# Two-layer graph block on one core: a fused tail for one more batch, and reordered statistics in the last part

## The chip, the cores and the metric

The kernel runs on one core of one Trainium2 chip. The metric is the device time of one execution in microseconds (us). A core has five engines that work side by side, each through its own in-order list of instructions: TensorE (PE in the profile; its weight loads are listed as PEld), VectorE (DVE), ScalarE (ACT), GpSimd (POOL) and SyncE (SP), which here only issues DMAs. They meet through semaphores: an instruction waits until the data that it reads are written and the buffer that it writes has been read out, and everything behind it on the same engine waits with it.

## The reference, cut to what matters

The input x has 128 batches of 128 rows by 512 columns, all in float32. There are two layers, each followed by a residual sum and a normalization over the 512 columns.

```python
# layer 0
A = einsum('od,bdn->bon', adj, x);  C = A + b          # same matrix twice
x = layernorm(x + max_over_columns(relu(A[..., None, :] + (C - A)[..., :, None])))
# layer 1: attention with 8 heads of 64 over the 128 rows of a batch
q, k, v = split(x @ w_qkv)
p = softmax(where(adj == 0, -inf, q @ k.T / 8))
o = (p @ v) @ w_proj + b_proj
x = layernorm(x + o + layernorm(o) * ln_gamma + ln_beta)
```

`layernorm(y)` is `(y - mean) / sqrt(var + 1e-5)`. For one batch the end of layer 1, called the tail below, is therefore: statistics of o, the inner normalization times gamma, two sums (with o, and with the output of layer 0 to which beta has been added already), statistics of that sum z, the outer normalization, and the store.

## The kernel before

Batches are worked in pairs (p counts pairs) and groups of four (g). A loop runs over the first 60 pairs; the rest, from `first = qk_unit(NG - 1, 0)` at line 951 to line 1194, is written out by hand, batch by batch. In it L is 127, the last batch, and LQ is 63, the last pair. The change lies in this last part only. The order of the calls in the source is the order of the instructions on each engine (`pin` keeps it), so moving a call moves all its instructions, on every engine that it uses.

**Matrix products.** The products with w_qkv and w_proj are done as units of seven block products in place of eight (`Unit`), over four PSUM banks b1 to b4. `product(i)` is a run of 8 matmul records on TensorE into the bank of that product (1, 6 and 7 use bank 1; 2 bank 2; 3 and 5 bank 3; 4 bank 4). `snap(k)` copies bank 1 to SBUF on ScalarE (line 186), and `result(half, col)` adds a bank and a snapshot on VectorE (line 199). `result(0, 1)` and `result(1, 1)` read bank 3. The next unit's product 5 goes into bank 3 again, so it waits for `result(0, 1)` of the unit before, and `snap(2)` reuses a buffer that the same result reads. `relay` and `relayed` (lines 191, 194) are copies on ScalarE that stand for some of the results in the last units, and `seed` (line 526) puts a bias into a bank. For the last four batches, `last_project` multiplies by the plain w_proj into a PSUM tile `pp`, which is o of that batch.

**Attention.** `scores` (tile pss), `softmax_max` (lines 405 and 417 on VectorE), `softmax_exp` (line 424, ScalarE, eight heads), `prob_out` (line 435 reciprocal, a multiply recorded at line 77, the transpose at line 445, and a DMA to DRAM from SP), `prob_read` (the DMAs back, line 465), `attend` (tile po) and `attend_copy` (line 495, ScalarE).

**Four ways to do a tail.** `stats` makes mean and variance on VectorE (`bn_stats` line 255, `bn_aggr` line 256), a negated mean (line 267) for those items that are not `fused`, and on GpSimd the variance plus epsilon (line 269), its power of -1/2 and the shift (both line 77); `columns` is its VectorE half without line 267, `finish_stats` the rest. The plain tail of a batch is `tail_inner_one` (ScalarE, line 278), `tail_residual_one` (three GpSimd instructions on 128x512: times gamma, plus o, plus the rest), statistics of z, and `tail_outer_one` (ScalarE and the store from SP, line 637). `scalar_stats` does the statistics of z on ScalarE instead (lines 665, 666, 669: per batch a pass for the sum, one for the squares), with three small GpSimd instructions in `finish_scalar_stats`. The fused tail does the middle on VectorE:

```python
def fused_open(b, mean):
    z_tile(b)      # z = (o - mean) * gamma;  rest = o + rest
    scalar_tensor_tensor(zs[b], o_of(b), mean, ga_bc, subtract, mult)    # line 624
    tt(nc.vector, rs_[b], o_of(b), rs_[b], add)                         # line 77
def fused_close(b):   # z = z * rs + rest
    scalar_tensor_tensor(z, z, rs, rs_[b], mult, add)                    # line 632
```

Before the change, batches 120 (L-7), 124 (L-3), 125, 126 and 127 take the fused tail, 121 (L-6), 122 and 123 the plain one. The very last outer normalization runs on VectorE (`tail_outer_vector`, line 653). Line 77 is the helper `tt` and line 74 the helper for matmuls, so many operations share these lines and are told apart by their tiles: `zl` holds z of the late batches (`z` and `xr` for some), `early` and `wlast` hold the rest, `s_o` the block sums for the second unit of w_proj, `st_mv_last`, `mv_last`, `rs_mv_last` and `sh_mv_last` the statistics, and `su`, `me`, `de` those of `scalar_stats`.

Of the kernel before, what the change touches and what calls it, by code (L numbers as in the profile page):

```python
# [16 lines left out]
def kernel(  # L17
# [58 lines left out]
    def tt(eng, dst, a, b, op):  # L76
        pin(eng.tensor_tensor(dst, a, b, op))  # L77
# [180 lines left out]
    def finish_stats(mv, keys, fused=0):  # L258


        n = len(keys)
        if n == 0:
            return
        part = slice(fused, n)
        sh = small.tile([P, NC], F32, tag="sh", name=f"sh_{mv.name}")
        if n > fused:
            pin(nc.vector.tensor_scalar(sh[:, part], mv[:, part, 0], -1.0, None, ALU.mult))
        rs = small.tile([P, NC], F32, tag="rs", name=f"rs_{mv.name}")
        pin(nc.gpsimd.tensor_scalar(rs[:, :n], mv[:, :n, 1], EPS, None, ALU.add))  # L269
        tt(nc.gpsimd, rs[:, :n], rs[:, :n], mhalf.to_broadcast([P, n]), ALU.pow)  # L270
        if n > fused:
            tt(nc.gpsimd, sh[:, part], sh[:, part], rs[:, part], ALU.mult)
        for k, key in enumerate(keys):
            stat_of[key] = rs[:, k : k + 1], sh[:, k : k + 1]

    def normalize(dst, src, key):
        rs, sh = stat_of.pop(key)
        pin(nc.scalar.activation(dst, src, AF.Identity, bias=sh, scale=rs))  # L278
# [140 lines left out]
    def softmax_exp(b, heads=range(H)):  # L419
        if 0 in heads:  # L420
            psums[b] = small.tile([P, H], F32, tag="sums", name=f"sums_{b}")
        for i in heads:
            pin(
                nc.scalar.activation(  # L424
                    prob[b][:, i],
                    prob[b][:, i],
                    AF.Exp,
                    bias=nmax[b][:, i : i + 1],
                    accum_out=psums[b][:, i : i + 1],
                )  # L430
            )
# [92 lines left out]
    def seed(unit, bank):  # L524
        bias = {1: bp_bc[:, :HE], 3: bd}[bank].unsqueeze(1).to_broadcast([P, 2, HE])
        pin(nc.scalar.copy(unit.new_bank(bank), bias))
# [37 lines left out]
    def tail_reload_to(q, place):  # L564
        pin(nc.sync.dma_start(out=place, in_=spill.pop(q)))
        for j in range(2):
            rs_[2 * q + j] = place[:, j]
# [33 lines left out]
    def z_tile(b):  # L601
        q, j = divmod(b, 2)
        tag, bufs = {58: ("xt", 2), 59: ("xt", 2), 60: ("z", 1), 61: ("qk0", 2)}.get(q, ("xs", 1))
        if tag == "xs":
            zs[b] = sb.tile([P, D], F32, tag=f"xs{b - B + G + 1}", name=f"z_{b}")
            return
        if q not in ends:
            ends[q] = sb.tile([P, 2, D], F32, tag=tag, name=f"zl_{q}", bufs=bufs)
        zs[b] = ends[q][:, j]

    def tail_inner_one(b):
        z_tile(b)
        normalize(zs[b], o_of(b), ("o", b))

    def tail_residual_one(b, steps=range(3)):
        for k in steps:
            with_, op = ((ga_bc, ALU.mult), (o_of(b), ALU.add), (rs_[b], ALU.add))[k]
            tt(nc.gpsimd, zs[b], zs[b], with_, op)

    def fused_open(b, mean):  # L620

        z_tile(b)
        pin(
            nc.vector.scalar_tensor_tensor(
                zs[b], o_of(b), mean, ga_bc, ALU.subtract, ALU.mult
            )
        )
        tt(nc.vector, rs_[b], o_of(b), rs_[b], ALU.add)

    def fused_close(b):  # L630
        z, (rs, _) = zs[b], stat_of.pop(("o", b))
        pin(nc.vector.scalar_tensor_tensor(z, z, rs, rs_[b], ALU.mult, ALU.add))
# [6 lines left out]
    def columns(name, *items):  # L639

        mv = small.tile([P, NC, 2], F32, tag="mv", name=f"mv_{name}")
        for k, (kind, b) in reversed(list(enumerate(items))):
            bn({"o": o_of, "z": zs.get, "y": xs.get}[kind](b), mv, k)
        return mv, items

    def stats(name, *items, fused=0):
        stat = columns(name, *items)
        finish_stats(*stat, fused)
        return stat[0]
# [6 lines left out]
    def scalar_stats(*batches):  # L656

        n, name = len(batches), f"{batches[0]}"
        trash = psum.tile([P, D], F32, tag="pss0", name=f"trash_{name}")
        sums, mean, dev = (  # L660
            small.tile([P, NC], F32, tag=f"{t}1", name=f"{t}1_{name}") for t in ("su", "me", "de")
        )
        act = nc.scalar.activation
        for k, b in enumerate(batches):
            pin(act(trash, zs[b], AF.Identity, accum_out=sums[:, k : k + 1]))
        pin(act(mean[:, :n], sums[:, :n], AF.Identity, scale=-1.0 / D))
        for k, b in enumerate(batches):
            pin(
                act(
                    trash, zs[b], AF.Square, bias=mean[:, k : k + 1], accum_out=dev[:, k : k + 1]  # L670
                )
            )
        return batches, mean, dev

    def finish_scalar_stats(stat):
        batches, sh, rs = stat
        n = len(batches)
        pin(nc.gpsimd.tensor_scalar(rs[:, :n], rs[:, :n], 1.0 / D, EPS, ALU.mult, ALU.add))
        tt(nc.gpsimd, rs[:, :n], rs[:, :n], mhalf.to_broadcast([P, n]), ALU.pow)
        tt(nc.gpsimd, sh[:, :n], sh[:, :n], rs[:, :n], ALU.mult)  # L680
        for k, b in enumerate(batches):
            stat_of["z", b] = rs[:, k : k + 1], sh[:, k : k + 1]
# [98 lines left out]
    for p in range(LAST):  # L781
        g, ph = divmod(p, 2)
        a, b = 2 * p, 2 * p + 1
        first = v_unit(0) if p == 0 else qk_unit(g + 1, ph)
# [3 lines left out]
        mv = small.tile([P, NC, 2], F32, tag="mv", name=f"mv_{p}")  # L788
# [152 lines left out]
    L = B - 1  # L941
# [3 lines left out]
    def prob_out(b):  # L945
        softmax_div(b)
        prob_transpose(b)
        prob_write(b)


    first = qk_unit(NG - 1, 0)
    mv = small.tile([P, NC, 2], F32, tag="mv", name=f"mv_{LAST}")
# [53 lines left out]
    early = sb.tile([P, 4, D], F32, tag="x1T", name="early", bufs=2)  # L1006
    for q in range(2):
        tail_reload_to(LQ - 4 + q, early[:, ds(2 * q, 2)])
    for t in (L - 13, L - 12):
        bn(o_of(t), mv, len(keys))  # L1010
        keys.append(("o", t))
    first.product(3)
    first.result(0, 1)
    softmax_exp(L - 4)
    prob_out(L - 5)
    for t in (L - 15, L - 14):
# [12 lines left out]
    before, o_u, v_u = second, o_unit(NG - 3), v_unit(NG - 1)  # L1029
# [47 lines left out]
    softmax_exp(L - 1, range(4))  # L1077
    o_u.product(3)
    v_u.product(2)
    prob_out(L - 2)  # L1080
    o_u.result(0, 1)
    softmax_exp(L - 1, range(4, H))
    v_u.relayed()
    softmax_max(L)
    v_u.product(6)
    v_u.snap(2)
    for t in (L - 9, L - 8):
        tail_inner_one(t)
        tail_residual_one(t)
    softmax_exp(L)  # L1090
    v_u.product(5)
    v_u.product(7)
    v_u.snap(3)
    v_u.product(4)
    stats("last_2", ("o", L - 11), ("o", L - 10))
    prob_out(L - 1)


    o_u = o_unit(NG - 2)
# [11 lines left out]
    o_u.product(1)  # L1111
    o_u.relay()
    v_u.product(3)
    for t in (L - 11, L - 10):
        tail_inner_one(t)
    prob_out(L)
    v_u.result(0, 1)
    o_u.product(2)
    o_u.relayed()
    seed(o_u, 3)  # L1120
    o_u.product(4)
    o_u.product(6)
    o_u.snap(2)
# [28 lines left out]
    last_project(L - 2, wlast)  # L1152
    for t in (L - 5, L - 4):
        tail_inner_one(t)
    mv = stats("last_5", ("o", L - 7), ("o", L - 6), fused=1)
    attend_copy(L - 1)
    attend_copy(L)
    last_project(L - 1, wlast)
    last_project(L, wlast)
    tail_inner_one(L - 6)  # L1160
    stat = scalar_stats(L - 11, L - 10)
    tail_residual_one(L - 5, [0, 1])
    fused_open(L - 7, mv[:, 0, 0:1])
    mv = stats("last_6", ("o", L - 3), fused=1)
    fused_open(L - 3, mv[:, 0, 0:1])
    fused_close(L - 7)
    fused_close(L - 3)
    tail_residual_one(L - 5, [2])
    finish_scalar_stats(stat)
    for t in (L - 11, L - 10):  # L1170
        tail_outer_one(t)
    tail_residual_one(L - 4, [0, 1])
    mv = stats("last_7", ("o", L - 2), ("z", L - 3), ("z", L - 7), fused=1)
    fused_open(L - 2, mv[:, 0, 0:1])
    fused_close(L - 2)
    tail_residual_one(L - 4, [2])
    for t in (L - 7, L - 3):
        tail_outer_one(t)
    stat = scalar_stats(L - 5, L - 4)
    tail_residual_one(L - 6, [0])  # L1180
    mv = stats("last_8", ("o", L - 1), ("z", L - 2), fused=1)
    fused_open(L - 1, mv[:, 0, 0:1])
    fused_close(L - 1)
    tail_residual_one(L - 6, [1, 2])
    finish_scalar_stats(stat)
    for t in (L - 2, L - 5, L - 4):
        tail_outer_one(t)
    mv = stats("last_9", ("o", L), ("z", L - 1), ("z", L - 6), fused=1)
    fused_open(L, mv[:, 0, 0:1])
    for t in (L - 1, L - 6):  # L1190
        tail_outer_one(t)
    fused_close(L)
    mv = stats("last_10", ("z", L), fused=1)
# [42 lines left out]
```

## Time and profile before

| what | us |
| --- | --- |
| timed runs, median of 3 | 1959.66 |
| lowest and highest of them | 1959.43, 1960.28 |
| the profiled execution, device time | 1959.19 |
| its span, first to last instruction | 1957.4 |
| granted TensorE clock, mean over the span | 0.996 |

The profiled execution is 0.47 us below the median of the timed ones, and 1.8 us of its time lie outside the span. Times inside the trace count from the start of the span. A line of the timeline gives start, duration, engine, source line, operation, the tile written and those read with their shapes, and in brackets how long the engine had been idle and what released it. Durations of one execution repeat closely for the same shape, so a duration well above that of its siblings is itself a finding.

### The profile page before, as it was taken

To read this page: it belongs to the slowest core of one execution; us is meant where nothing else is said; L and a number is where in the kernel's file an instruction comes from. 1 tells how busy PE (TensorE), PEld (TensorE's weight loads), DVE (VectorE), ACT (ScalarE), POOL (GpSimd) and SP (SyncE) were. 2 spreads that over 40 slices of the span, in tenths; PEclk is the share of its full clock that TensorE was granted. 3 is DMA by queue.
4 is the path that set the end of the run, shared out by engine and by line. 5 is a ranking of instruction groups with operands and counts; after the bars stand their busy time and mean duration, and the time that the engine had idled before them with its cause. 6 is when DMAs were issued, how large, how long until landed. Compare 5 with 4: busy or idle time off the path is not lost.

```text
span 1957.4 us, 33035 instructions
## 1 busy us (share of the span) xinstructions
PE 1932.5 (99%) x11533; PEld 1635.9 (84%) x11533; DVE 1562.1 (80%) x2514; ACT 1065.3 (54%) x3094; POOL 1296.3 (66%) x821
## 2 busy tenths in 40 slices
PE   9999999999999999999999999999999999999996
PEld 6888888888888888888888888888888888888884
DVE  6767878778778788787787787887877878878786
ACT  3444655555545546555555465565554554655575
POOL 6336766767667676667676676766676766767748
PEclk9999999999999999999999999999999999999998
DMA  7747566576566665666765756757667657567464
GB/s 223 170 121 188 145 185 180 160 199 162 168 189 166 178 192 157 190 166 168 205 159 165 199 153 186 189 158 193 166 167 201 161 169 195 156 188 180 133 220 136
DMA packets 444934, 341.74 MB, mean 175 GB/s; under 512 B 276832, under 2 KB 378336, under 8 KB 444768
## 3 DMA queue, kind: packets, MB, share of 16 engines
q1 hardware_dynamic: 444336, 338.85, 64.0%
q8 instruction: 91, 1.49, 0.3%
q10 hardware_dynamic: 432, 0.79, 0.1%
q14 instruction: 75, 0.61, 0.1%
HBM read 172.82 MB, written 166.72 MB: 173 GB/s over the span
## 4 chain that ended last, share of the span: by engine, by line
PE 94%; DVE 3%; POOL 2%; ACT 1%; issue 0%; POOLq 0%; ACTq 0%; DVEq 0%
PE b_qk L74 39%; PE b_v L74 19%; PE b_o L74 18%; PE pss L74 6%; PE po L74 6%; PE pa L74 5%; POOL zl L77 1%; DVE s L77 0%; DVE pu L445 0%; ACT s L424 0%; DVE st_mv_last L255 0%; DVE amax L291 0%; POOL rs_mv_last L77 0%; POOL s_o L77 0%; DVE s L405 0%
## 5 line engine op out<-in xcount | busy, mean ns | idle before, releaser
L74 PE MATMUL b_qk<-s_x,wqk 128*128 128x256 f32 x2048 | 473.8, 379 | 1.6 <-DVE qk L199 1.4
L74 PEld LDWEIGHTS b_qk<-s_x,wqk 128*128 128x128 f32 x2048 | 388.8, 190 | 56.0 <-DVE qk L199 2.2
L424 ACT ACTIVATE s<-s,nmax 128x128 f32<-128x128 f32 x1024 | 396.1, 391 | 3.9 <-DVE nmax L417 3.9
L74 PE MATMUL b_qk<-x1T,wqk 128*128 128x256 f32 x1536 | 358.9, 383 | 0.1
L74 PEld LDWEIGHTS b_qk<-x1T,wqk 128*128 128x128 f32 x1536 | 286.6, 190 | 45.3 <-issue 1.0
L77 POOL TENSOR_TENSOR z<-z,ga_bc 128x1024 f32<-128x1024 f32 x58 | 164.6, 2838 | 167.9 <-ACT z L278 167.9
L269 POOL TENSOR_SCALAR rs_mv<-mv 128x6 f32<-128x6 f32 (+2 forms) x61 | 14.7, 241 | 386.7 <-DVE mv L256 386.7
L77 DVE TENSOR_TENSOR s<-s,rec 128x1024 f32<-128x1024 f32 x128 | 253.1, 1977 | 4.4
L186 ACT COPY u_qk<-b_qk 128x512 f32<-128x512 f32 x192 | 112.3, 585 | 242.7 <-PE b_qk L74 241.8
L74 PE MATMUL b_v<-wv,s_x 128*128 128x256 f32 x1024 | 237.0, 379 | 0.9 <-DVE o L199 0.9
L74 PE MATMUL b_o<-wp,s_o 128*128 128x256 f32 x992 | 229.4, 379 | 0.7 <-POOL s_o L77 0.7
L74 PEld LDWEIGHTS b_v<-wv,s_x 128*128 128x128 f32 x1024 | 194.4, 190 | 27.8 <-DVE o L199 1.3
L405 DVE SCALAR_TENSOR_TENSOR s<-pss,mask 128x512 f32<-128x512 f32 x256 | 164.3, 683 | 61.3 <-PE pss L74 61.2
L74 PEld LDWEIGHTS b_o<-wp,s_o 128*128 128x128 f32 x992 | 188.2, 190 | 26.9 <-POOL s_o L77 1.1
L199 DVE TENSOR_TENSOR qk<-b_qk,u_qk 128x512 f32<-128x512 f32 x256 | 168.0, 675 | 49.8 <-PE b_qk L74 45.8
L77 POOL TENSOR_TENSOR x<-x,be_bc 128x1024 f32<-128x1024 f32 x64 | 181.3, 2833 | 33.1 <-DVE rec L435 27.4
L424 ACT ACTIVATION_READ_ACCUMULATOR s<-s,nmax 128x1 f32 x1024 | 194.4, 190 | 0.0
L199 DVE TENSOR_TENSOR v<-b_v,u_v 128x512 f32<-128x512 f32 x127 | 86.2, 680 | 133.6 <-PE po L74 128.8
L186 ACT COPY u_o<-b_o 128x512 f32<-128x512 f32 x91 | 53.3, 585 | 241.8 <-PE b_o L74 241.8
L186 ACT COPY u_v<-b_v 128x512 f32<-128x512 f32 x95 | 55.6, 585 | 234.7 <-PE b_v L74 233.4
L74 PE MATMUL b_v<-wv,x1T 128*128 128x256 f32 x768 | 176.5, 379 | 0.0
L74 PEld LDWEIGHTS b_v<-wv,x1T 128*128 128x128 f32 x768 | 145.8, 190 | 32.3 <-issue 13.9
(128 smaller groups left out, 3399.2 us busy)
## 6 DMA issues: line engine op xcount, KB each, us to landing
hop<-pu SPq DMA_DIRECT2D x128, 512.0 KB, 3.7
pT<-hop SPq DMA_DIRECT2D x512, 128.0 KB, 3.7
spill<-x SPq DMA_DIRECT2D x64, 512.0 KB, 4.8
x<-in_x_dram SPq DMA_DIRECT2D x62, 512.0 KB, 4.5
xhop<-xt SPq DMA_DIRECT2D x248, 128.0 KB, 2.3
x1T<-xhop SPq DMA_DIRECT2D x248, 128.0 KB, 3.9
xr<-spill SPq DMA_DIRECT2D x59, 512.0 KB, 3.6
out_dram<-xr SPq DMA_DIRECT2D x58, 512.0 KB, 4.1
```

The source lines that it names most:

```text
L74: pin(nc.tensor.matmul(*args, **kwargs))
L77: pin(eng.tensor_tensor(dst, a, b, op))
L186: pin(nc.scalar.copy(t, self.banks[1]))
L199: nc.vector.tensor_tensor(self.out[half, col], self.banks[bank], self.snaps[k], ALU.add)
L269: pin(nc.gpsimd.tensor_scalar(rs[:, :n], mv[:, :n, 1], EPS, None, ALU.add))
L405: nc.vector.scalar_tensor_tensor(s[:, par], pss[b][par], SCALE, mask.unsqueeze(1).to_broadcast([P, NP, P]), ALU.mult, ALU.add,)
L424: nc.scalar.activation(prob[b][:, i], prob[b][:, i], AF.Exp, bias=nmax[b][:, i : i + 1], accum_out=psums[b][:, i : i + 1],)
```

## The change

The first edits are moves. In three places `result(0, 1)` or a statistic changes its place among the VectorE instructions; in one, two tail inners and residuals go ahead of `product(6)` and `snap(2)`; in one, `stats` is cut into `columns` and a later `finish_stats`. The second half rewrites the end: the batch with index L-6 = 121 (the 122nd) takes the fused tail, `scalar_stats` of batches 122 and 123 is done one batch at a time, the GpSimd steps of 122 and 123 are placed anew, and the statistics of z of 121 move from `last_9` to `last_8`. The statistics of the last two batches (o of 127, z of 126) thus stand alone in `last_9`. No function is new.

```diff
+    first.product(3)
+    first.result(0, 1)
     for t in (L - 13, L - 12):
         bn(o_of(t), mv, len(keys))
         keys.append(("o", t))
-    first.product(3)
-    first.result(0, 1)
     softmax_exp(L - 4)
...
     softmax_exp(L - 1, range(4))
     o_u.product(3)
     v_u.product(2)
+    o_u.result(0, 1)
     prob_out(L - 2)
-    o_u.result(0, 1)
     softmax_exp(L - 1, range(4, H))
     v_u.relayed()
     softmax_max(L)
-    v_u.product(6)
-    v_u.snap(2)
     for t in (L - 9, L - 8):
         tail_inner_one(t)
         tail_residual_one(t)
+    v_u.product(6)
+    v_u.snap(2)
     softmax_exp(L)
...
-    stats("last_2", ("o", L - 11), ("o", L - 10))
+    stat = columns("last_2", ("o", L - 11), ("o", L - 10))
     prob_out(L - 1)
...
     v_u.product(3)
-    for t in (L - 11, L - 10):
-        tail_inner_one(t)
+    finish_stats(*stat)
     prob_out(L)
     v_u.result(0, 1)
     o_u.product(2)
     o_u.relayed()
     seed(o_u, 3)
+    for t in (L - 11, L - 10):
+        tail_inner_one(t)
     o_u.product(4)
     o_u.product(6)
     o_u.snap(2)
...
-    mv = stats("last_5", ("o", L - 7), ("o", L - 6), fused=1)
+    mv = stats("last_5", ("o", L - 7), ("o", L - 6), fused=2)
     attend_copy(L - 1)
     attend_copy(L)
     last_project(L - 1, wlast)
     last_project(L, wlast)
-    tail_inner_one(L - 6)
     stat = scalar_stats(L - 11, L - 10)
-    tail_residual_one(L - 5, [0, 1])
+    tail_residual_one(L - 5, [0])
     fused_open(L - 7, mv[:, 0, 0:1])
-    mv = stats("last_6", ("o", L - 3), fused=1)
-    fused_open(L - 3, mv[:, 0, 0:1])
+    mv1 = stats("last_6", ("o", L - 3), fused=1)
+    tail_residual_one(L - 5, [1, 2])
+    fused_open(L - 3, mv1[:, 0, 0:1])
     fused_close(L - 7)
     fused_close(L - 3)
-    tail_residual_one(L - 5, [2])
     finish_scalar_stats(stat)
     for t in (L - 11, L - 10):
         tail_outer_one(t)
-    tail_residual_one(L - 4, [0, 1])
+    stat5 = scalar_stats(L - 5)
+    fused_open(L - 6, mv[:, 1, 0:1])
     mv = stats("last_7", ("o", L - 2), ("z", L - 3), ("z", L - 7), fused=1)
     fused_open(L - 2, mv[:, 0, 0:1])
+    fused_close(L - 6)
     fused_close(L - 2)
-    tail_residual_one(L - 4, [2])
+    tail_residual_one(L - 4)
     for t in (L - 7, L - 3):
         tail_outer_one(t)
-    stat = scalar_stats(L - 5, L - 4)
-    tail_residual_one(L - 6, [0])
-    mv = stats("last_8", ("o", L - 1), ("z", L - 2), fused=1)
+    mv = stats("last_8", ("o", L - 1), ("z", L - 2), ("z", L - 6), fused=1)
     fused_open(L - 1, mv[:, 0, 0:1])
     fused_close(L - 1)
-    tail_residual_one(L - 6, [1, 2])
-    finish_scalar_stats(stat)
-    for t in (L - 2, L - 5, L - 4):
+    finish_scalar_stats(stat5)
+    stat4 = scalar_stats(L - 4)
+    for t in (L - 6, L - 2, L - 5):
         tail_outer_one(t)
-    mv = stats("last_9", ("o", L), ("z", L - 1), ("z", L - 6), fused=1)
+    finish_scalar_stats(stat4)
+    mv = stats("last_9", ("o", L), ("z", L - 1), fused=1)
     fused_open(L, mv[:, 0, 0:1])
-    for t in (L - 1, L - 6):
+    for t in (L - 4, L - 1):
         tail_outer_one(t)
     fused_close(L)
```

## The prediction

> **What bounds the kernel now.** I read the page's shares and chain first, then the windows of the last 90 us, then the timeline around each edit, one engine at a time.
>
> ```profile
> PE 1932.5 (99%) x11533; PEld 1635.9 (84%) x11533; DVE 1562.1 (80%) x2514; ACT 1065.3 (54%) x3094; POOL 1296.3 (66%) x821
> PE 94%; DVE 3%; POOL 2%; ACT 1%; issue 0%; POOLq 0%; ACTq 0%; DVEq 0%
> ...
> 1900.00:1928.00 28.00, 27.27 (x175) 21.61 (x175) 23.63 (x41) 17.08 (x40) 26.05 (x26) 1.00 0.58 169
> 1928.00:1940.00 12.00, 11.62 (x46) 5.36 (x42) 8.53 (x16) 7.83 (x17) 10.85 (x17) 1.00 0.25 94
> 1940.00:1957.40 17.40, 0.00 (x0) 0.00 (x0) 10.26 (x22) 8.43 (x16) 10.08 (x15) 0.55 0.33 121
> ```
>
> TensorE carries 94% of the chain, so over most of the span only its waits can be gained. The end is another matter: GpSimd is busy 26.05 of 28 us from 1900 and 10.85 of 12 from 1928, and after 1940 TensorE has nothing left, while VectorE and GpSimd (10.26 and 10.08 of 17.40) hand statistics to each other. What the change can move is a few TensorE waits before 1915 and this exchange.
>
> ```profile
> 1866.81 0.66 DVE L199 TENSOR_TENSOR qk<-b_qk,u_qk 128x512 f32<-128x512 f32 x1
> 1867.52 1.99 PE L74 MATMUL b_qk<-s_x,wqk 128*128 128x256 f32 x8 [0.56 <-DVE qk L199]
> ...
> 1898.64 0.65 DVE L199 TENSOR_TENSOR o<-b_o,u_o 128x512 f32<-128x512 f32 x1
> 1899.35 0.92 PE L74 MATMUL b_v<-wv,s_x 128*128 128x256 f32 x3 [0.93 <-DVE o L199]
> 1899.38 0.58 ACT L186 COPY u_v<-b_v 128x512 f32<-128x512 f32 x1 [1.37 <-DVE o L199]
> 1899.87 0.82 ACT L278 ACTIVATE zl<-o,sh_mv_last,rs_mv_last 128x512 f32<-128x512 f32 x1
> ...
> 1900.76 1.27 POOL L77 TENSOR_TENSOR zl<-zl,ga_bc 128x512 f32<-128x512 f32 x1 [2.47 <-ACT zl L278]
> ...
> 1903.70 2.11 DVE L77 TENSOR_TENSOR s<-s,rec 128x1024 f32<-128x1024 f32 x1
> 1904.69 2.27 POOL L77 TENSOR_TENSOR zl<-zl,ga_bc 128x512 f32<-128x512 f32 x1
> ...
> 1914.53 0.70 PE L74 MATMUL b_o<-wp,s_o 128*128 128x256 f32 x2 [0.73 <-POOL s_o L77]
> ...
> 1932.97 1.75 DVE L632 SCALAR_TENSOR_TENSOR z<-z,rs_mv_last,wlast 128x512 f32<-128x512 f32 x1 [2.02 <-POOL rs_mv_last L77]
> ...
> 1947.15 0.69 DVE L255 BATCH_NORM_STATS2 st_mv_last<-zl 128x6 f32<-128x512 f32 x1 [2.50 <-POOL zl L77]
> ...
> 1953.85 0.55 DVE L653 TENSOR_SCALAR z<-z,mv_last,rs_mv_last 128x512 f32<-128x512 f32 x1 [1.01 <-POOL rs_mv_last L77]
> ```
>
> The reader should see three TensorE waits (0.56, 0.93, 0.73); a ScalarE copy that waits 1.37 for the same result and holds up the first tail inner, and so GpSimd; and two late VectorE waits for GpSimd, of which 2.50 is for z of batch 121. Durations also show a collision: the divide (`s<-s,rec`) takes 1.23 at 1896.21 but 2.11 beside GpSimd, and the GpSimd product behind it 2.27 in place of 1.27.
>
> **What the Trainium skill says.** "SBUF — State Buffer", section "SBUF: two separate sides", calls the port pair of VectorE and GpSimd "an exclusive lock, not a bandwidth split": a VectorE instruction with two SBUF inputs and a GpSimd instruction exclude each other for their whole length, whoever starts first. The trace agrees: 1903.70 plus 2.11 less 1.23 is 1904.58, where the GpSimd sum from 1903.46 ends (1904.73). Sums that read a PSUM tile (`pp`, 0.68) show no such delay. So closing a fused tail (`z,rs,rest`, all SBUF) excludes GpSimd, and for batch 121, whose o lies in SBUF, opening it should too.
>
> **The change part by part.** Each number is laid on the order of instructions per engine in the built program; all gains count from the trace of before.
>
> *First move: bank 3 result before two statistics (1865).* VectorE is free for it at 1865.28, and the product that it reads is the first half of the run of 16 matmuls at 1863.35 (3.62), so done at about 1865.2. TensorE's wait of 0.56 goes; the statistics come 0.6 later on VectorE but end at the same time. I see no later wait that takes it back: VectorE waits 2.12 for `pss` at 1881.37, ScalarE 2.91 before 1884.19, and both shift. Gain 0.56.
>
> *Second move: `o_u.result(0,1)` before the softmax output (1896), and tail inners before `snap(2)`.* The result starts at 1895.42 instead of 1898.64, so TensorE's 0.93 goes too. VectorE's sum of work is unchanged. ScalarE is free at 1898.01 less 0.56 = 1897.45; the shift of batches 118 and 119, its small power slowed to 1.73 by a divide before, still has to wait for one and comes at 1897.6. The first inner runs at 1897.63 instead of 1899.87, GpSimd's residuals start at 1898.52 instead of 1900.76: 2.24 earlier. The price: `snap(2)` is now behind two inners of 0.76, ends at 1899.73, and product 7 waits about 0.25.
>
> *Third: `finish_stats` of 116 and 117 behind the block sums, their inners behind `seed`.* GpSimd does six residuals from 1898.52 (about 1.35 each, one blocked by a divide for 1.1) until 1907.4, four `s_o` sums (the second blocked until 1909.65 by the last divide) until 1913.6, and three small steps (1.29) until 1914.9. The sum that product 6 awaits ends at 1910.9, before TensorE asks (1912.6), so the 0.73 goes. But the inners now start at 1914.96, not 1911.93, and ahead of the next `snap(2)`, which ends at 1917.08; product 7 of this unit needs it and starts at 1917.12 instead of 1917.99. Of the TensorE gain 0.87 is left, of GpSimd's 1.04 (residual of 116 at 1915.85 instead of 1916.89). Removing the shift multiply of `last_5` saves 0.2 more on GpSimd.
>
> *Fourth: the tail.* Removed: inner of 121 on ScalarE (0.82), three GpSimd residuals (1.27, 1.71, 1.27), VectorE's wait of 2.50. Added on VectorE: open 0.77, sum 0.68, close 0.77; on ScalarE one more mean (0.20); on GpSimd a second triple of small steps (about 1.1). My schedule: statistics of 120 and 121 ready at 1925.35, `last_6` at 1927.65; close 120 at 1929.1, close 124 blocked by a GpSimd sum until 1932.57 (before 1934.72); open 121 blocked again by the last residual of 122, ending 1934.27, its sum 1934.9; three statistics until 1937.2 (before 1937.05). So the 2 us won at close 124 pay for the new work, here. Then GpSimd, which before was busy with residuals of 123 and took this set only at 1938.50, is idle and starts it at 1937.3; close 121 follows at 1938.75 beside it, close 125 is blocked by the first residual of 123 until 1941.22 (before 1940.51); three statistics (now with 121) until 1943.55, close 126 ends 1945.77 (before 1944.65), two statistics until 1947.38. Here the 2.50 wait and one set of statistics are gone. GpSimd's two triples end at 1947.87, its step for 127 at 1948.95, close 127 1949.75, statistics 1950.68, last steps 1951.63, final instruction 1951.67 instead of 1953.85. Sum: 2.18 earlier. The stores on SP are six of the same size in nearly the old order; batch 121's leaves two places earlier, and the last one still follows VectorE, so they cost nothing.
>
> *Unknown: does opening 121 exclude GpSimd?* No row of before shows one squarely against a residual; at 1926.30 such an opening (0.77) overlaps a small GpSimd step that took its usual 0.22. Ends: 0 (it excludes, as in the sum) and 0.9 (no block at 1932.55). I take the middle, 0.45.
>
> Gain 2.18 + 0.45 = 2.6. Against the profiled execution that is 1959.19 - 2.6 = 1956.6; the median of the runs is 0.47 higher, so 1957.0.
>
> **The rivals.** *The whole lead survives.* If the last divide doesn't block the second `s_o`, the small steps end 1.2 earlier, `snap(2)` is in time, and TensorE and GpSimd keep about 2.1; with 0.9 for the opening, 2.2 + 1.2 + 0.9 = 4.3: 1955.4. For it: the blocks depend on tenths of a us. Against: the divide took 2.33 at 1908.41 before, so GpSimd is dense there. *The lead is eaten.* Later `snap(2)` and blocks on each divide leave 0.3 of 1.04, and the longer VectorE list in the tail is blocked once more (0.75): 2.2 - 0.75 - 0.75 = 0.7: 1959.0. For it: VectorE's statistics in the tail are no earlier in my schedule (1937.2 against 1937.05). *Slower: VectorE becomes the bound of the tail by port exclusion.* Place: from opening 121 to closing 125, five two-SBUF instructions against three residuals of 123. If the lead of 1.04 is lost and the sum and close of 121 each wait a full residual (1.1), 2.2 - 1.04 - 2.2 = -1.0: 1960.6. It decides once more than two further blocks of a residual's length fall on VectorE. Against: GpSimd's residuals of 123 stand behind the statistics that VectorE must finish first, so most of the time there is nothing to collide with.
>
> **How the numbers follow.** Forecast 0.45, own range 1955.9 to 1958.6; whole lead 0.28; eaten 0.19; slower 0.08. The range 1954.5 to 1959.8 takes in the first three and leaves out most of the slower case. Faster or slower counts beyond 0.2%, 3.9 us, about what a measurement of this kernel can tell from no change: under 1955.7 lie most of the whole-lead case and a little of the forecast, 0.31; over 1963.6 only a tail of the slower case, 0.03; within, 0.66.
>
> **What would show it.** No TensorE wait for `qk` near 1867 nor for `o` near 1899; GpSimd's first `zl` two us earlier; a new TensorE wait for `u_o` before attention of batch 124, and a GpSimd idle of 1 to 2 us for `mv_last` where 123's residuals stood. It is wrong if `pss` of batch 124 doesn't come 0.5 earlier, if TensorE's last matmul ends no earlier than 1939.6, or if the last closes take over 1.2 us each.

## The result, and the profile after

| | before | after |
| --- | --- | --- |
| median of 18 timed runs each, us | 1959.49 | 1956.29 |
| lowest and highest | 1958.69, 1960.44 | 1955.61, 1958.70 |
| ratio, 95% interval | | 0.9984 [0.9977, 0.999] |
| profiled execution, us | 1959.19 | 1958.70 |
| last part (defined below), us | 92.25 | 89.30 |

The medians differ by 3.20 us, 0.16%. The profiled execution, the longest of its 18 runs, shows only 0.49 of it, for reasons that lie far ahead of the first edit. The page's first part and chain of after, beside those that the prediction shows, and from its timeline the first late instructions:

```profile
PE 1933.8 (99%) x11533; PEld 1637.0 (84%) x11533; DVE 1563.4 (80%) x2516; ACT 1065.1 (54%) x3094; POOL 1294.9 (66%) x820
...
PE 94%; DVE 2%; POOL 2%; ACT 1%; DMA 1%; issue 0%; SPq 0%; POOLq 0%; ACTq 0%; DVEq 0%
```

```profile
6.88 1.12 PE L74 MATMUL pa<-x,adjT 128*128 128x512 f32 x2 [0.66 <-DMA x<-in_x_dram]
...
14.62 1.99 PE L74 MATMUL b_qk<-x1T,wqk 128*128 128x256 f32 x8
...
19.83 4.99 PE L74 MATMUL b_qk<-x1T,wqk 128*128 128x256 f32 x16
...
24.66 3.62 PE L74 MATMUL b_qk<-s_x,wqk 128*128 128x256 f32 x16
```

The shares can't tell the two kernels apart. One entry is new in the chain: DMA has 1%, where before had none. In this execution the first loads of x came late, which makes 0.40 us: the product at 14.62 started at 14.22 before. Then the granted TensorE clock drops: it is 0.55 from 19 to 21 us and 0.60 from 21 to 23, where before has 1.00 in both, and the 16 matmuls at 19.83 take 4.99 where those of before, at 19.12, took 3.75. The product at 24.66 is thus 1.95 later (22.71 before). The last half us comes at 78.45, where TensorE waits 0.55 for a load of `pT`, which before has not. From there to the first edit the distance stays the same. Both programs are identical in all of this, and in the second execution of after (e12) the first of these products is even early (13.84), while the clock is again 0.55 and 0.60. So I compare only the **last part**: from the start of the VectorE instruction `s<-pss,mask` ahead of the first edit (1862.15 before, 1864.61 after, a shift of 2.46) to the end of the last VectorE instruction (1954.40 and 1953.91). It is 92.25 long before and 89.30 after, 2.95 shorter. Times of after that are called aligned have 2.46 taken off. The same instructions in both timelines, aligned:

| start of (unless "end" is said) | before | after, aligned | difference |
| --- | --- | --- | --- |
| TensorE scores of batch 124 read by VectorE (line 405) | 1881.37 | 1880.70 | -0.67 |
| first GpSimd product of batch 118 (`zl<-zl,ga_bc`) | 1900.76 | 1898.34 | -2.42 |
| TensorE attention of batch 122 (`po`) | 1904.73 | 1903.14 | -1.59 |
| TensorE product 1 of the w_proj unit | 1906.63 | 1905.59 | -1.04 |
| TensorE product 6 | 1914.53 | 1912.60 | -1.93 |
| GpSimd product of batch 116 | 1916.89 | 1915.21 | -1.68 |
| TensorE attention of batch 124 | 1919.90 | 1918.35 | -1.55 |
| VectorE opening of 120 (line 624) | 1926.30 | 1925.75 | -0.55 |
| VectorE close of 124 (line 632), end | 1934.72 | 1931.73 | -2.99 |
| statistics `last_7`, end | 1937.13 | 1936.41 | -0.72 |
| close of 125 | 1939.73 | 1938.38 | -1.35 |
| close of 126 | 1943.88 | 1944.13 | +0.25 |
| statistics `last_9`, end | 1949.65 | 1946.65 | -3.00 |
| last instruction (line 653), end | 1954.40 | 1951.45 | -2.95 |

The lead is won, lost and won again: it is 2.42 at the first GpSimd product of batch 118, 0.55 at the opening of 120, nothing at the close of 126, and 3.0 at the end. The timeline of after shows where (unaligned times):

```profile
1865.80 5.34 PE L74 MATMUL b_qk<-s_x,wqk 128*128 128x256 f32 x24
...
1898.33 4.11 PE L74 MATMUL b_v<-wv,s_x 128*128 128x256 f32 x17
...
1900.80 1.28 POOL L77 TENSOR_TENSOR zl<-zl,ga_bc 128x512 f32<-128x512 f32 x1 [0.93 <-ACT zl L278]
...
1906.10 2.13 POOL L77 TENSOR_TENSOR zl<-zl,o 128x512 f32<-128x512 f32 x1
...
1908.05 1.99 PE L74 MATMUL b_o<-wp,oT 128*128 128x256 f32 x8 [0.48 <-ACT b_o L526]
...
1910.89 2.13 POOL L77 TENSOR_TENSOR s_o<-s_o,oT 128x512 f32<-128x512 f32 x1
...
1915.06 3.62 PE L74 MATMUL b_o<-wp,s_o 128*128 128x256 f32 x16
...
1916.79 1.52 ACT L278 ACTIVATE zl<-o,sh_mv_last,rs_mv_last 128x512 f32<-128x512 f32 x2 [2.13 <-POOL sh_mv_last L77]
...
1917.67 1.27 POOL L77 TENSOR_TENSOR zl<-zl,ga_bc 128x512 f32<-128x512 f32 x1 [0.93 <-ACT zl L278]
...
1918.92 1.97 PE L74 MATMUL b_o<-wp,s_o 128*128 128x256 f32 x8 [0.24 <-ACT u_o L186]
...
1924.55 1.27 POOL L77 TENSOR_TENSOR zl<-zl,o 128x512 f32<-128x512 f32 x1
1924.60 1.24 DVE L267 TENSOR_SCALAR sh_mv_last<-mv_last 128x2 f32<-128x2 f32 x1
...
1933.72 1.60 POOL L77 TENSOR_TENSOR zl<-zl,wlast 128x512 f32<-128x512 f32 x1
...
1934.11 1.75 DVE L624 SCALAR_TENSOR_TENSOR zl<-o,mv_last,ga_bc 128x512 f32<-128x512 f32 x1
...
1938.96 0.23 POOL L269 TENSOR_SCALAR rs_mv_last<-mv_last 128x3 f32<-128x3 f32 x1 [1.66 <-DVE sh_mv_last L267]
...
1940.17 0.74 DVE L632 SCALAR_TENSOR_TENSOR zl<-zl,rs_mv_last,early 128x512 f32<-128x512 f32 x1
...
1940.84 0.74 DVE L632 SCALAR_TENSOR_TENSOR z<-z,rs_mv_last,wlast 128x512 f32<-128x512 f32 x1
...
1944.12 1.27 POOL L77 TENSOR_TENSOR zl<-zl,wlast 128x512 f32<-128x512 f32 x1
...
1946.59 0.78 DVE L632 SCALAR_TENSOR_TENSOR z<-z,rs_mv_last,wlast 128x512 f32<-128x512 f32 x1 [1.21 <-POOL rs_mv_last L77]
...
1953.36 0.55 DVE L653 TENSOR_SCALAR z<-z,mv_last,rs_mv_last 128x512 f32<-128x512 f32 x1 [1.00 <-POOL rs_mv_last L77]
```

The reader should see four things. The three TensorE waits of before are gone (24 matmuls at 1865.80 and 17 at 1898.33 in one run, and no bracket at product 6, 1915.06); in their place are 0.48 for the bias copy `seed` and 0.24 for `u_o`. ScalarE and GpSimd stand idle until 1916.79 and 1917.67 for the statistics of 116 and 117, which the third move made late. Two VectorE instructions are far too long: 1.24 for a pass over 128x2 that takes 0.17 elsewhere, and 1.75 for the opening of batch 121 (0.77 for that of batch 120, with the same operands); each lies beside a GpSimd instruction. And the wait of 2.50 for z of batch 121 is gone, while the close of 126 now waits 1.21 for statistics that GpSimd takes up only after a residual of batch 123 (the sum at 1944.12).

### The profile page after: what moved, and what is told of

The parts are those of the page before. It is cut to its first block, busy times and chain, and to the rows that moved or that the text cites. A ratio compares the mean times of both kernels' runs of the same rounds, so it can differ in the third digit from the quotient of the medians.

```text
span 1957.0 us, 33035 instructions
## 1 busy us (share of the span) xinstructions
PE 1933.8 (99%) x11533; PEld 1637.0 (84%) x11533; DVE 1563.4 (80%) x2516; ACT 1065.1 (54%) x3094; POOL 1294.9 (66%) x820
## 4 chain that ended last, share of the span: by engine, by line
PE 94%; DVE 2%; POOL 2%; ACT 1%; DMA 1%; issue 0%; SPq 0%; POOLq 0%; ACTq 0%; DVEq 0%
PE b_qk L74 39%; PE b_v L74 19%; PE b_o L74 18%; PE pss L74 6%; PE po L74 6%; PE pa L74 5%; POOL zl L77 1%; DVE st_mv_last L255 0%; ACT s L424 0%; POOL s_o L77 0%; DMA x<-in_x_dram 0%; DMA pT<-hop 0%; POOL rs_mv_last L77 0%; DMA hop<-pu 0%; DVE amax L291 0%
```

## The experiments

Eleven kernels were run. For each I give the last part from its profiled execution (start of the same line-405 instruction to the end of line 653) and the median and ratio of its timed runs, against the kernel before on the same chip. The interval of a ratio is 2.5 to 4 us wide, and most effects here are smaller, so the verdicts on single edits rest on the last part. The last kernel, the kernel after once more, shows how well it repeats: 89.32 against 89.30, although the two executions differ in their start-up. In all eleven, the median differs from that of before by the same amount as the last part, within 0.5 us. A smaller effect of a single edit therefore rests on one profiled execution of its kernel.

### One part alone

**e1: only the first move, on the kernel before.**

```diff
+    first.product(3)
+    first.result(0, 1)
     for t in (L - 13, L - 12):
...
-    first.product(3)
-    first.result(0, 1)
     softmax_exp(L - 4)
```

> The kernel before with the first move alone (result(0,1) of bank 3 ahead of the statistics of batches 114 and 115). Measure: the last part, from the start of the first masked score sum of batch 123 on VectorE (line 405) to the end of the last VectorE instruction (line 653); before 92.25 us, after the whole change 89.30. Theory (a TensorE wait removed moves everything behind it): the wait of 0.56 for qk is gone and the last part is 91.6, with masked sums of batch 124 0.67 earlier. Rival (the end is set by GpSimd and VectorE, the lead is absorbed): the sums of 124 come earlier but the last part stays at 92.1 to 92.3.

Measured: last part 91.63, 0.62 less than before; median 1959.37 against 1959.91, ratio 0.9996 [0.9988, 1.0005]. The timed runs alone would settle nothing. The last part is what the theory said (91.6); with its run of 24 matmuls without a gap it agrees with the gain of 0.56 that the prediction counted, kept to the end.

**e2: all moves ahead of the tail, with the old tail.** The diff is that of the change down to the inners of L-11 and L-10.

> All moves of the first half, the tail from batch 127's attention on as before. Theory (the lead of the front reaches the end whole): GpSimd's residuals of 117 end 1.65 earlier as in the whole change, and the last part is 90.6. Rival (tail absorbs it, VectorE's small instruction waiting for GpSimd): lead at the residuals 1.65, but the last part 91.3 or more. Third (the front does nothing without the new tail): 92.2.

Measured: 91.17, 1.08 less than before; median 1958.47 against 1959.91, ratio 0.9994 [0.9986, 1.0002]. That lies between the theory (90.6) and the rival (91.3 or more): the old tail takes the lead back in part. Its timeline:

```profile
1922.79 1.27 POOL L77 TENSOR_TENSOR zl<-zl,o 128x512 f32<-128x512 f32 x1
1922.84 1.25 DVE L267 TENSOR_SCALAR sh_mv_last<-mv_last 128x2 f32<-128x2 f32 x1
...
1929.97 1.27 POOL L77 TENSOR_TENSOR zl<-zl,o 128x512 f32<-128x512 f32 x1
1930.02 1.77 DVE L632 SCALAR_TENSOR_TENSOR zl<-zl,rs_mv_last,early 128x512 f32<-128x512 f32 x1
```

Both VectorE instructions start 0.05 after a GpSimd sum and last until that sum is over and they have run. Before, the first started 0.05 ahead of the sum, in a gap between two (0.17), and the second met only the end of one (1.07). The moves shifted the phase between the engines, and the shift makes these two instructions 1.1 and 0.7 longer. The end loses less: GpSimd's lead at the product of batch 116 is 1.66, that of the last instruction 1.08.

**e3: only the new tail, on the old moves.** The diff is the rest of the change, from `last_5` on.

> The kernel before with the rewritten tail alone (batch 121 fused, statistics of 122 and 123 apart). Theory (gains add): 92.25 - 1.3 = 90.95, VectorE's wait of 2.50 for z of 121 gone. Rival (the fused tail only pays because the front brings GpSimd a lead): 92.0 or more. Other rival (the tail is the whole of it): 89.5.

Measured: 90.86, 1.39 less than before; median 1958.08 against 1959.91, ratio 0.9992 [0.9984, 1.0]. The expectation was 90.95. Here `last_4` meets nothing (0.17), but the opening of 121 takes 1.75 as in after. e2 and e3 together make 2.47 of the 2.95; the other 0.5 is interplay, presumably because the new tail uses a lead that the old one wasted.

### The two moves around `snap(2)` and the statistics of 116 and 117

**e4: after, with `product(6)` and `snap(2)` ahead of the inners of 118 and 119 again.**

```diff
     softmax_max(L)
+    v_u.product(6)
+    v_u.snap(2)
     for t in (L - 9, L - 8):
         tail_inner_one(t)
         tail_residual_one(t)
-    v_u.product(6)
-    v_u.snap(2)
```

> The whole change, but product(6) and snap(2) of v_u again ahead of the two tail inners of 118 and 119. Theory: the first residual on GpSimd comes about 0.6 later (one ScalarE copy), TensorE loses no wait for u_v, and the last part is 89.3 to 89.9. Rival (this order is what gives GpSimd its lead): 90.9 or more.

Measured: 90.43, 1.13 more than after; median 1958.06 against 1959.91, ratio 0.999 [0.9984, 0.9997]. A miss for both: I expected 89.3 to 89.9, and the rival was 90.9 or more. The copy that now stands ahead of the inner waits 0.46 for product 6, so GpSimd's first product comes 0.84 later and not 0.6:

```profile
1900.17 1.28 POOL L77 TENSOR_TENSOR zl<-zl,ga_bc 128x512 f32<-128x512 f32 x1 [1.75 <-ACT zl L278]
...
1903.96 1.27 DVE L77 TENSOR_TENSOR s<-s,rec 128x1024 f32<-128x1024 f32 x1
...
1904.11 2.26 POOL L77 TENSOR_TENSOR zl<-zl,ga_bc 128x512 f32<-128x512 f32 x1
...
1909.03 2.25 POOL L77 TENSOR_TENSOR s_o<-oT 128x512 f32<-128x512 f32 x1
...
1918.54 1.97 PE L74 MATMUL b_o<-wp,s_o 128*128 128x256 f32 x8 [1.32 <-ACT u_o L186]
```

The divide started 0.15 before the GpSimd product, so GpSimd waits until it is over, and again at 1909.03. After also has two such meetings, of 2.13 each (1906.10 and 1910.89), so they add only 0.25. The delay, 1.09 together, reaches the small steps of 116 and 117 and, since the third move put those ahead of the next `snap(2)`, TensorE: it waits 1.32 for `u_o` where after waits 0.24. So putting the inners first is worth 1.1 with the third move in place; without it, that was not tried.

**e5: after without the third move.**

```diff
-    stat = columns("last_2", ("o", L - 11), ("o", L - 10))
+    stats("last_2", ("o", L - 11), ("o", L - 10))
     prob_out(L - 1)
...
-    finish_stats(*stat)
+    for t in (L - 11, L - 10):
+        tail_inner_one(t)
...
     seed(o_u, 3)
-    for t in (L - 11, L - 10):
-        tail_inner_one(t)
```

> The whole change without its third move (statistics of 116 and 117 finished at once, their inners ahead of relayed, as before). Last part after the change 89.30 us. Theory of the prediction (block sums first remove TensorE's wait for s_o, but the later inners hold up snap(2) and leave GpSimd idle 0.9): the lead of 2.4 on GpSimd already brings the second s_o in time, so nothing is lost and up to 0.7 won, 88.6 to 89.4. Rival (the third move carries part of the gain): 89.8 to 90.5, with a TensorE wait for s_o again.

Measured: 88.42, 0.88 *less* than after and just under the theory's range; median 1956.00 against 1959.39, ratio 0.998 [0.9973, 0.9988]. By the medians the gain over after is only 0.2 to 0.5, which they can't tell from 0.88. Its timeline at the place:

```profile
1913.36 5.34 PE L74 MATMUL b_o<-wp,s_o 128*128 128x256 f32 x24
...
1914.44 1.27 POOL L77 TENSOR_TENSOR zl<-zl,ga_bc 128x512 f32<-128x512 f32 x1
...
1915.28 0.58 ACT L186 COPY u_o<-b_o 128x512 f32<-128x512 f32 x1 [1.92 <-PE b_o L74]
...
1918.63 1.97 PE L74 MATMUL po<-pT,v 128*64 128x128 f32 x32
...
1921.31 1.28 POOL L77 TENSOR_TENSOR zl<-zl,o 128x512 f32<-128x512 f32 x1
...
1922.42 0.20 DVE L267 TENSOR_SCALAR sh_mv_last<-mv_last 128x2 f32<-128x2 f32 x1
```

Product 6 doesn't wait for `s_o`, though the small steps stand ahead of the sums again: the second move alone brings GpSimd there in time. `snap(2)` waits only for its product, TensorE runs 24 matmuls without a gap, and GpSimd starts the product of 116 without idling. The third move removes a wait that the second had removed already, and adds two.

Of these two, TensorE's 0.24 is not what reaches the end: e5 has another wait in its place (0.33 for `v` at 1908.07), and its attention of batch 124 is no earlier (1918.63, which is 1920.94 on the clock of after, against 1920.81). GpSimd is 0.92 earlier. VectorE comes to the pass of `last_4` 0.13 later than in after, but GpSimd's sum is then nearly over, and the pass takes 0.20 in place of 1.24; so the opening of 120 comes 0.87 earlier, and everything behind it keeps that. The 0.88 is therefore GpSimd's lead together with a block that it dissolves. What the lead is worth without the block was not tried; the block taken away by giving the pass to GpSimd gains nothing (e8, below).

### The shared ports in the tail

**e6: after, with gamma for the opening of 121 read from a copy in PSUM.** `fused_open` takes it as a third argument, in place of `ga_bc`.

```diff
+    ga_ps = psum.tile([P, D], F32, tag="pss1", name="ga_ps")
+    pin(nc.scalar.copy(ga_ps, ga_bc))
...
-    fused_open(L - 6, mv[:, 1, 0:1])
+    fused_open(L - 6, mv[:, 1, 0:1], ga_ps)
```

> The whole change, with gamma copied once to PSUM by ScalarE (0.58, ahead of the last projections) and read from there by the opening of batch 121 alone, so that this instruction has one SBUF input in place of two. Theory (it took 1.75 because it and the last residual of 122 on GpSimd exclude each other): the opening takes 0.75 to 0.8, the sum behind it is blocked for some 0.3, statistics of z of 120 start 0.6 to 0.9 earlier, last part about 88.7. Rival (the 1.75 is a wait for something else, or scalar operand): it stays at 1.7.

Measured: 88.71, as the theory said, and 0.59 less than after; median 1955.98 against 1959.39, ratio 0.998 [0.9973, 0.9988]. VectorE's timeline:

```profile
1933.16 0.74 DVE L624 SCALAR_TENSOR_TENSOR zl<-o,mv_last,ga_ps 128x512 f32<-128x512 f32 x1
...
1933.82 1.10 DVE L77 TENSOR_TENSOR early<-o,early 128x512 f32<-128x512 f32 x1
```

The same instruction beside the same GpSimd sum takes 0.74 in place of 1.75 once only one of its operands lies in SBUF. So its long duration was the block of the shared ports, and not the shape or a late operand. The sum behind it, with two SBUF operands, meets the rest of the GpSimd instruction and gives back 0.42 of the 1.0.

**e8: after, with the negated means of `last_4` on GpSimd** (the 1.24 at 1924.60). `stats` hands `neg` on to the pass at line 267.

```diff
-    stats("last_4", ("o", L - 5), ("o", L - 4))
+    stats("last_4", ("o", L - 5), ("o", L - 4), neg=nc.gpsimd)
```

> The whole change, with the negated means of last_4 (two numbers per row) made on GpSimd instead of VectorE. Theory (this VectorE instruction took 1.24 instead of 0.17 because a single-source SBUF instruction on VectorE and a GpSimd sum exclude each other, and delays everything behind it by 1.0): result(0,1), the statistics and the opening of 120 come 1.0 earlier; of that 0.3 to 0.9 reaches the end, last part 88.4 to 89.0. Rival (VectorE has slack there, since closes 120 and 124 wait for GpSimd anyway): 89.2 to 89.5.

Measured: 89.85, 0.55 *more* than after; median 1957.01 against 1959.39, ratio 0.9988 [0.9981, 0.9995]. Again a miss for theory and rival. The opening of 120 comes 1.0 earlier, but then:

```profile
1929.40 1.43 DVE L632 SCALAR_TENSOR_TENSOR zl<-zl,rs_mv_last,early 128x512 f32<-128x512 f32 x1
...
1931.61 1.75 DVE L632 SCALAR_TENSOR_TENSOR z<-z,rs_mv_last,wlast 128x512 f32<-128x512 f32 x1 [0.78 <-POOL rs_mv_last L77]
```

The close of 120 now meets a GpSimd product (1.43; 0.74 in after), GpSimd's own small steps come later for it, and the close of 124 waits 0.78 and is blocked all the same. So moving the pass off VectorE does not help. That its 1.24 is a block, the other kernels show: the pass takes 1.24 in after and 1.25 in e2, where it starts 0.05 behind the start of a GpSimd sum, 0.20 in e5, where it starts 0.17 ahead of a sum's end, and 0.17 before, where it starts in a gap.

### The close of 126

**e7: after, with another order of `last_8`, 123's residual and `last_9`.** The third GpSimd instruction of 123's residual goes behind the statistics that the close of 126 needs.

```diff
-    tail_residual_one(L - 4)
+    tail_residual_one(L - 4, [0, 1])
...
     fused_close(L - 1)
+    tail_residual_one(L - 4, [2])
     finish_scalar_stats(stat5)
-    stat4 = scalar_stats(L - 4)
-    for t in (L - 6, L - 2, L - 5):
+    for t in (L - 6, L - 2):
         tail_outer_one(t)
-    finish_scalar_stats(stat4)
+    stat4 = scalar_stats(L - 4)
+    tail_outer_one(L - 5)
...
-    for t in (L - 4, L - 1):
+    finish_scalar_stats(stat4)
+    for t in (L - 1, L - 4):
```

> The whole change with another order on GpSimd and ScalarE in the last 15 us: statistics last_8 ahead of the third residual step of 123, last_9 ahead of finish_scalar_stats of 123, ScalarE's statistics of 123 after the outers of 121 and 125. Theory (VectorE's wait of 1.21 before close 126 is GpSimd's residual of 123, and 127's step waits for the triple of 123): close 126 starts 1.2 earlier, close 127 1.3 earlier, last part 88.0. Rival (GpSimd's residual then collides with close 126 and ScalarE's statistics of 123 become the end): 89.0 or more.

Measured: 89.18, only 0.12 less than after; median 1956.22 against 1959.39, ratio 0.9985 [0.9978, 0.9992]. The theory said 88.0, and the rival (89.0 or more) came, by the collision that it named:

```profile
1944.25 1.83 DVE L632 SCALAR_TENSOR_TENSOR z<-z,rs_mv_last,wlast 128x512 f32<-128x512 f32 x1
1944.27 1.27 POOL L77 TENSOR_TENSOR zl<-zl,wlast 128x512 f32<-128x512 f32 x1
```

The wait of 1.21 is gone, and the close takes 1.83 in place of 0.78: the residual that had stood ahead of it in GpSimd's list now runs beside it. The wait became a block of nearly the same length.

**e10: e5 and e6 together; e11: e10 with the order of e7, but 123's last residual also behind the three small steps of 122.** Against e7:

```diff
     fused_close(L - 1)
-    tail_residual_one(L - 4, [2])
     finish_scalar_stats(stat5)
+    tail_residual_one(L - 4, [2])
```

> The whole change without its third move and with gamma from PSUM for the opening of 121. Theory (the two act at different places, 1912 to 1919 and 1931 to 1936, and add): last part 88.42 - 0.59 = 87.8. Rival (both only shift which instruction of VectorE meets which of GpSimd, so that sums don't hold): anything from 87.9 to 89.0.

> As the run before, with the order of e7_order, but the third residual step of 123 behind the small triple of 122 rather than straight behind the statistics, so that close 126 (1.83 in e7_order) finds GpSimd with small steps only. Theory: close 126 takes 0.8 to 1.2 and starts without the wait of 1.21, last part 86.8 to 87.2. Rival (small steps and the close exclude each other as well, or close 127 is held up by the later triple of 123): 87.6 or more.

Measured: e10 87.82, e11 86.85, both as their theories said; medians 1955.30 and 1953.79 against 1959.24, ratios 0.9978 [0.997, 0.9987] and 0.9973 [0.9962, 0.9983]. The gains of e5 and e6 add (0.88 + 0.59 = 1.47; measured 1.48). In e11 GpSimd has small steps beside the close of 126:

```profile
1940.83 0.75 DVE L632 SCALAR_TENSOR_TENSOR z<-z,rs_mv_last,wlast 128x512 f32<-128x512 f32 x1
...
1940.98 0.65 POOL L678 TENSOR_SCALAR de<-de 128x1 f32<-128x1 f32 x1
...
1942.47 1.26 POOL L77 TENSOR_TENSOR zl<-zl,wlast 128x512 f32<-128x512 f32 x1
...
1947.75 0.55 DVE L653 TENSOR_SCALAR z<-z,mv_last,rs_mv_last 128x512 f32<-128x512 f32 x1 [1.15 <-POOL rs_mv_last L77]
```

There is no wait and no block at 1940.83. The two still exclude each other, but the close starts first, and it is the small GpSimd step at 1940.98 that is held up (0.65, where the next of its kind takes 0.19). The residual follows at 1942.47, beside statistics. e11 is the best version found: 5.45 less than before and 2.56 less than after in the same set of runs, where the last part says 5.40 and 2.45.

**e12: after once more, beside e10 and e11.**

> The changed kernel once more, to see how far the last part of one execution repeats. Theory (the order of collisions is fixed once the program runs in step): 89.3 within 0.1. Rival (tenths of a us decide collisions anew each time): off by 0.5 or more.

Measured: 89.32, within the theory's 0.1; median 1956.35 against 1959.24, ratio 0.9985 [0.9979, 0.9992].

## Why the prediction was right, point by point

The forecast was a gain of 2.6; the last part shows 2.95 and the medians 3.20. Direction, mechanism and size hold, and 1956.29 lies in the forecast's own range, 0.7 under its centre; 0.17 of that is that the median of before was 1959.49 in these runs and not 1959.66. But the sum came out well partly because errors on single terms cancelled.

- **First move, 0.56.** Right: 0.62 alone (e1), and nothing took it back.
- **Second move, GpSimd 2.24 earlier.** 2.42. The shift's product was held up by a divide as foreseen (1.01 at 1898.86). TensorE kept 1.04 at product 1, with a new wait of 0.48 for `seed` that the prediction did not name.
- **Third move, counted as what removes the 0.73 for `s_o` and keeps 0.87 of TensorE's lead.** This step failed. Its forecast signs all appeared (0.24 for `u_o`, a late inner), but its balance had the wrong sign, because I did not work out whether the second move alone brings `s_o` in time. It does, and the third move costs 0.88 (e5), by GpSimd's idle time and the collision that follows, and not by the TensorE wait that I had weighed. After it, GpSimd was 1.68 ahead at the residual of 116 where I had 1.04: its blocks by divides were overestimated, the direction that the rival "the whole lead survives" pointed to.
- **Opening and close of 120.** The opening gained 0.55: a block of 1.07 on the 128x2 pass of `last_4` ate the rest and was in no term of the sum. The Trainium skill, "SBUF — State Buffer", section "Who interferes with whom", lists `tensor_scalar` among the VectorE operations that can, if their operands meet certain conditions, contend with GpSimd for the shared ports even with one SBUF source; the trace agrees (1.24 against 0.17; in which mode the pass ran it doesn't show), and I had applied the rule only to instructions with two.
- **Close of 124.** Blocked, as forecast, but ended 2.99 earlier and not 2.15.
- **"Unknown: does opening 121 exclude GpSimd?"** I took the middle, 0.45. It excludes: 1.75. The term should have been 0, and e6 measures what its absence is worth, 0.59 and not 0.9. The skill's sentence on two SBUF inputs stood in the prediction and answered it. So did the trace of before, one row below the one that I read: the small step at 1926.34 kept its 0.22, but the next one, under the same opening, took 1.00 where the same step takes 0.71 at 1928.18:

```profile
1926.30 0.77 DVE L624 SCALAR_TENSOR_TENSOR zl<-o,mv_last,ga_bc 128x512 f32<-128x512 f32 x1
...
1926.65 1.00 POOL L77 TENSOR_TENSOR rs_mv_last<-rs_mv_last,mhalf 128x2 f32<-128x2 f32 x1
```

- **Close of 125, forecast as blocked.** It wasn't (0.74): it started before GpSimd's product, which took the longer time in its place (1.78 at 1940.93). The close of 125 therefore ended 2.1 earlier than in my schedule (1939.12 aligned, 1941.22 forecast).
- **Close of 126, forecast to end 1945.77.** It ended at 1944.91 aligned, after a wait of 1.21 for statistics behind a residual of 123. That wait was in no step. It gave back 1.2 of the 2.1 that the close of 125 had won.
- **The end.** The 2.50 wait and one set of statistics went as forecast; the last instruction started at 1950.90 aligned, where the schedule had 1951.67 before the 0.45 was added on top. So the schedule was 0.77 too late and the unknown 0.45 too generous; together 0.3.

Of the signs named in advance, all came: scores of batch 124 0.67 earlier, TensorE's last matmul at 1938.18 aligned (1939.63 before), GpSimd idle 1.66 at 1938.96, the last closes 0.74 to 0.78. The slower rival needed more than two further blocks on VectorE; after the opening of 121 there was none. (It counted five two-SBUF instructions from that opening to the close of 125; there are four, since the opening of 125 and its sum read `pp`.)

What stays open: the 0.5 by which the two halves gain more together than apart was followed only to e2's blocks, and not taken apart further; and in e5, how much of the 0.88 the block of `last_4` makes and how much GpSimd's lead.

## What to carry to other kernels

Where two engines exclude each other for the length of an instruction, an edit is worth what it saves plus what its shift makes or breaks of such meetings: list for each two-SBUF instruction what the other engine runs beside it, and look again after every move (e7 and e8 each removed a delay and met another). Work out each move also on top of the others, since a wait that one has removed can't be removed again by the next, while its price stays. To separate such waits, put short steps of the other engine beside the instruction that must not be blocked, which then lose the time (e11), or give it an operand in PSUM (e6).

## What the runs showed that I had not expected

- A VectorE pass over 128x2 can cost 1.24 us: it takes 0.17 alone, but waits out a GpSimd sum of 128x512 in which it happens to fall (after, and again 1.25 in e2).
- Who waits is decided by less than 0.2 us: in e4 the divide started 0.15 ahead of the GpSimd product, which took 2.26; in e2 the close of 120 started 0.05 behind the sum and took 1.77.
- Two executions of kernels that are identical up to 1860 us differed by 2.46 us there: 0.40 from late loads of x, about 1.5 from a granted clock of 0.55 and 0.60 at 19 to 23 us, 0.5 from a load at 78 us. A profile's span should be compared from an instruction ahead of the change, not from zero.
